# First gather of a deformable convolution: positions made in two halves, and the second image's table copy and normalized image stored later, from another queue

## The chip, the cores and the metric

The kernel runs on one core of a Trainium2 chip. The metric is device time in microseconds, from the launch of the program to its end. Engines are named as in the profile: PE is TensorE (PEld its weight loads), DVE is VectorE, ACT is ScalarE, POOL is GpSimd, SP is the sync engine, which here only issues transfers. SPq, ACTq and POOLq are the issuing sides of these engines.

## The reference

Four layers run one after another on an input of 4 images, 192 channels, 64x64 pixels, all in float32. The change touches the beginning of layer 0, a transformer block whose query is a 3x3 deformable convolution. Cut to that part:

```python
xs = x.reshape(B, C, H * W).transpose(0, 2, 1)
xn = layer_norm(xs, gamma1, beta1).transpose(0, 2, 1).reshape(B, C, H, W)
q = deform_conv(xn, w_p, b_p, w_d)
...
def deform_conv(x, w_p, b_p, w_d):
    off = conv2d(x, w_p, stride=1, pad=1) + b_p[None, :, None, None]
    xp = jnp.pad(x, ((0, 0), (0, 0), (1, 1), (1, 1)))
    ...
    px = off[:, :N].transpose(0, 2, 3, 1) + p0x + pn[0]
    py = off[:, N:].transpose(0, 2, 3, 1) + p0y + pn[1]
    fx, fy = jnp.floor(px), jnp.floor(py)
    ...
    xo = g_lt * gat(qlx, qly) + g_rb * gat(qrx, qry) + g_lb * gat(qlx, qry) + g_rt * gat(qrx, qly)
    return conv2d(xo, w_d, stride=KS, pad=0)
```

A small convolution gives every pixel two offsets for each of nine taps. At each of these nine places the normalized, padded image is read with bilinear weights from four neighbours, all 192 channels at once, and the result goes into a second convolution. The rest of layer 0 is channel attention and an MLP. Layer 1 is a non-local block, layer 2 a window attention block, layer 3 a small masked depthwise convolution.

## The kernel before, in words

**Order of the work.** One Python function describes all work as tiles and instructions. A scheduler then orders the instructions of each engine by their place in the program and by its own estimate of when operands are ready, and it sets the semaphores. Each engine runs its own list strictly in order. `in_turn(...)` (L174) pins a transfer behind the instruction that was described last for the same engine, so that the scheduler can't issue it earlier. Transfers that SP issues go out in SP's order, those that ACT issues in ACT's.

**Images.** Image 0 is prepared and gathered at the very beginning (L1948 to L1965). Its gather runs beside the making of constants (`constants`, L183) and beside the preparation of image 1 (`offsets(1, second, woven=True)`). Then follows the MLP of image 0 (`mlp0(0, ...)`, L1970). After it a loop over the four images runs layers 1, 2 and 3 of image b. Inside layer 1 of image b the gather of image b+1 is woven in, and inside layer 3's stage the MLP of image b+1. Images 2 and 3 are prepared at the start of layer 1 of the image before them (L1986).

**`offsets` (L436)** prepares one image in four steps:

- It normalizes the image in eight chunks into `xn` (96 partitions, two channel halves, a padded image of 66x66).
- `write_table` (L489) transposes pixels to rows and stores them into `table`, an array in DRAM with one entry of 2x192 floats for every padded pixel. The row of a pixel is stored twice: into columns C to 2C of its own entry (q = 1), and into columns 0 to C of the entry one image row (66 entries) later (q = 0). One entry then holds two pixels that stand above each other, and two entries in a row hold the four neighbours that the bilinear read needs. Image 0 and images 2 and 3 do this in 4 groups, image 1 in 8. Each group issues four stores on SP (two q by two image rows, L509). For image 0 the transposed rows also stay in SBUF in `kept`.
- After the groups, `xn` is stored as a whole to `xn_drams` (L512, 3270 KB). The MLP of that image reads it from there (`load_normalized`, L757).
- `convolve` (L514) computes the offsets in two halves of 16 tiles each (72 matmuls of 512 columns a half), and adds the grid into `pos` (L535). After both halves nine VectorE instructions (L544 to L556) clamp the positions, take floors, make the weights `pos` and `fr`, and make the index `idx`, each over all 32 tiles of 18 values.

Image 1 runs `convolve` before `write_table`, the others the other way round.

**`gather` (L559)** goes over five groups of taps (two, two, two, two, one), and in each over the 32 tiles. For each tile and tap POOL issues one indirect transfer (L616) that fetches 128 times four neighbours, 393 KB, into one of 11 slots of `ring`. Then ACT (L622), DVE (L623), ACT (L626), DVE (L627) interpolate, and PE multiplies `xo` with the unshifted row of the pixels (`kept`, or `ti` loaded from columns C to 2C of the table, L610). At the end come the second convolution, the attention matrix, and its product with the projection, `m2`; the last ACT instructions of it are the copies at L728 and L729.

**`mlp0` (L739)** then takes one pixel chunk after another: `attend`, the sum with the image, a layer norm whose squares ACT makes at L812, two matmul layers with a GELU between them.

**Buffers.** `xn`, `ring` and other large tiles share two buffers of the pool `big`; a new one waits until all readers of the one before are done, a store to DRAM too. There are two tables and two copies of `xn_drams`, used by even and odd images.

Of the kernel before, what the change touches and what calls it, by code (L numbers as in the profile page):

```python
# [13 lines left out]
ALU = mybir.AluOpType  # L14
# [67 lines left out]
def conv_seq_kernel(ctx: ExitStack, tc: tile.TileContext, a, out: bass.AP):  # L82
# [350 lines left out]
    def given(b):  # L433
        return a["x"][b].rearrange("(k p) h w -> p k (h w)", p=P)

    def offsets(b, pool, kept=None, woven=False):  # L436

# [16 lines left out]
        with ExitStack() as s:  # L456
            sb = s.enter_context(pool_of(name="l0a", bufs=1 if woven else 2))
            s1 = s.enter_context(pool_of(name="l0a1", bufs=1))
            ps = s.enter_context(pool_of(name="l0aps", bufs=2, space=PSUM))
            for i in range(NCH):  # L460
                xi = sb.tile([P, 2, CN], F32, tag="xi", name=f"xi_{b}_{i}", bufs=2)
                nc.sync.dma_start(out=xi, in_=given(b)[:, :, bass.ts(i, CN)])
                layer_norm(
                    xi, CN, xnv[:, :, 1 + 8 * i : 9 + 8 * i, 1:65], sb, ps, f"l0_{b}_{i}",
                    affine=(V["l0_g1"], V["l0_b1"]), rows=8,
                )
                yield

            wp = s1.tile([P, 2, 9, 32], F32, tag="wp", name=f"wp_{b}")
            given_wp = s1.tile([P, 2, 9, 18], F32, tag="given_wp", name=f"given_wp_{b}")  # L470
            nc.sync.dma_start(out=given_wp, in_=a["wp"].rearrange("(k p) t o -> p k t o", p=P))
            nc.gpsimd.memset(wp, 0.0)
            nc.gpsimd.tensor_copy(wp[:, :, :, 0:18], given_wp)
            bp = s1.tile([128, 1], F32, tag="bp", name=f"bp_{b}")
            nc.gpsimd.memset(bp, 0.0)
            for q in range(4):
                nc.sync.dma_start(out=bp[32 * q : 32 * q + 18, :], in_=a["bp"])
            p0 = s1.tile([128, NU, 18], F32, tag="p0", name=f"p0_{b}")
            for to, of, t in (((0, W), (0, W), 0), ((W, 2 * W - 2), (WP, 2 * W), 0), ((2 * W - 2, 2 * W), (0, 2), 1)):
                nc.sync.dma_start(out=p0[slice(*to), 0, :], in_=a["p0"][slice(*of), t, :])  # L480
            n = 1
            while n < NU:
                nc.gpsimd.tensor_scalar_add(p0[:, n : 2 * n, 0:9], p0[:, 0:n, 0:9], 2.0 * n)
                nc.gpsimd.tensor_copy(p0[:, n : 2 * n, 9:18], p0[:, 0:n, 9:18])
                n *= 2

            G, T = 4 if woven else 8, 4

            def write_table():  # L489
                for g in range(NU // G):  # L490
                    if kept is None:
                        tt = sb.tile([128, G, C], F32, tag="tt", name=f"tt_{b}_{g}", bufs=2)
                    else:
                        tt = kept[:, bass.ts(g, G)]
                    for j in range(G):
                        r0 = 2 * (g * G + j) + 1
                        pt = ps.tile([128, C], F32, tag="tr", name=f"pt_{b}_{g}_{j}")
                        for k in range(2):
                            for h in range(2):
                                nc.tensor.matmul(  # L500
                                    pt[bass.ts(h, W), bass.ts(k, P)], lhsT=xnv[:, k, r0 + h, 1 : W + 1], rhs=ident[:P, :P],
                                    start=True, stop=True,
                                )
                        nc.scalar.copy(tt[:, j, :], pt)
                    for q in range(2):
                        e = g * G * UT + (2 - q) * WP + 2
                        to = table[e : e + G * UT, bass.ts(q, C)].rearrange("(j r w) c -> r w j c", r=2, w=WP)
                        for h in range(2):
                            nc.sync.dma_start(out=to[h, 0:W], in_=tt[bass.ts(h, W)])  # L509
                    if not woven or g % 2 == 1:  # L510
                        yield
                nc.sync.dma_start(out=xn_drams[b % 2], in_=xn)  # L512

            def convolve():  # L514
                for g0 in range(0, NU // T, 4):
                    ng, m = 4, 128
                    po = ps.tile([128, T * 128], F32, tag="off", name=f"po_{b}_{g0}", bufs=1)
                    for tap in range(9):
                        for k in range(2):
                            for q in range(ng):  # L520
                                r0, c0 = (g0 + q) * 2 * T + tap // 3, tap % 3
                                nc.tensor.matmul(
                                    po[32 * q : 32 * q + 32].rearrange("p (r c) -> p r c", c=W), lhsT=wp[:, k, tap, :],
                                    rhs=xnv[:, k, r0 : r0 + 2 * T, c0 : c0 + W],
                                    start=tap == 0 and k == 0, stop=tap == 8 and k == 1,
                                )
                    ot = sb.tile([128, T * 128], F32, tag="ot", name=f"ot_{b}_{g0}")
                    nc.scalar.activation(ot[:m], po[:m], AF.Identity, bias=bp[:m])
                    pp = ps.tile([128, T, 4, 32], F32, tag="tr", name=f"pp_{b}_{g0}")
                    for j in range(T):  # L530
                        nc.tensor.transpose(
                            pp[:, j, 0:ng, :].rearrange("p q o -> p (q o)"), ot[:m, bass.ts(j, 128)], ident[:m, :m]
                        )
                    tiles = slice(g0 * T, (g0 + ng) * T)
                    nc.vector.tensor_tensor(  # L535
                        pos[:, tiles, :].rearrange("p (q j) o -> p j q o", j=T), pp[:, :, 0:ng, 0:18],
                        p0[:, tiles, :].rearrange("p (q j) o -> p j q o", j=T), ALU.add,
                    )
                    yield

            for part in (convolve(), write_table()) if woven else (write_table(), convolve()):
                yield from part

            nc.vector.tensor_scalar(pos, pos, -1.0, 65.0, ALU.max, ALU.min)  # L544
            fi = s1.tile([128, NU, 18], I32, name=f"fi_{b}", tag="fi")
            fl = s1.tile([128, NU, 18], F32, name=f"fl_{b}", tag="fl")
            nc.vector.tensor_copy(fi, pos)
            nc.vector.tensor_copy(fl, fi)
            nc.vector.tensor_tensor(fr, fl, pos, ALU.is_gt)
            nc.vector.tensor_tensor(fl, fl, fr, ALU.subtract)  # L550
            nc.vector.tensor_tensor(fr, pos, fl, ALU.subtract)
            nc.vector.tensor_scalar(pos, fr, -1.0, 1.0, ALU.mult, ALU.add)
            nc.vector.scalar_tensor_tensor(
                fl[:, :, 0:9], fl[:, :, 0:9], float(WP), fl[:, :, 9:18], ALU.mult, ALU.add
            )
            nc.vector.tensor_scalar(idx, fl[:, :, 0:9], 2.0, 2.0 * MID, ALU.mult, ALU.add)  # L556
        return pos, fr, idx

    def gather(b, s, at, m2, kept=None):  # L559
# [1387 lines left out]

    begun, at_second = ExitStack(), None  # L1948
    second = begun.enter_context(pool_of(name="l0second", bufs=1))
    with ExitStack() as s:  # L1950
        sb = s.enter_context(pool_of(name="l0first", bufs=1))
        m2 = stats.tile([M, C + 3 * M], F32, tag="m2", name="m2_0")
        kept = sb.tile([128, NU, C], F32, tag="kept", name="kept")
        at = links(offsets(0, sb, kept))
        beside = [constants(), offsets(1, second, woven=True)]
        for k, _ in enumerate(gather(0, s, at, m2, kept)):
            if k < 20 or not beside:
                continue
            if len(beside) == 2 and k % 4 == 0 or len(beside) == 1 and k % 13 == 0:
                try:  # L1960
                    next(beside[0])
                except StopIteration as end:
                    at_second = end.value
                    beside.pop(0)
        assert not beside  # L1965
    with ExitStack() as s:
        sb, pool = (s.enter_context(pool_of(name=n, bufs=1)) for n in ("norms0", "l0d0"))
        ps = s.enter_context(pool_of(name="l0dps", bufs=2, space=PSUM))
        wide = s.enter_context(pool_of(name="l0dps2", bufs=5, space=PSUM))
        for _ in mlp0(0, m2, pool, sb, Psums({"n": ps, "v": ps, "h": wide})):  # L1970
            pass
# [117 lines left out]
```

## Time and profile before

| | us |
|---|---|
| median of 4 runs | 6745.02 (6739.23 to 6752.7) |
| the profiled execution | 6748.98 |
| its span, first to last instruction | 6747.2 |
| preparation of image 0, up to the first gather | 0 to 123.9 |
| gather of image 0, first to last issue | 123.9 to 609.0 |
| its end, up to the last copy into `m2` | 609.0 to 643.4 |
| MLP of image 0 | 642.5 to 837 |
| first gather of image 1, inside layer 1 of image 0 | 841.5 |
| first gathers of images 2 and 3 | 2483.1 and 4057.4 |

The table is read off the timeline of the profiled execution. Some groups of its page that belong to the gather (line, engine, operation, output and input, how many over the whole run; then busy us and mean ns, and idle us before them with what ended most of it):

```profile
L616 POOL DMA_INDIRECT ring<-table,idx x1152 | 1634.4, 1419 | 1149.3 <-issue 221.1
L622 ACT ACTIVATE row<-ring,pos 128x384 f32<-128x384 f32 x1152 | 671.9, 608 | 202.9 <-DVE xo L627 106.3
L623 DVE SCALAR_TENSOR_TENSOR row<-ring,fr,row 128x384 f32<-128x384 f32 x1152 | 675.1, 613 | 93.9 <-ACT row L622 64.8
L634 PE MATMUL h<-kept,xo 128*128 128x192 f32 x960 | 249.2, 396 | 125.5 <-DVE xo L627 79.9
```

A quarter of each of the first three counts belongs to image 0. In the tables of stretches that follow below, the DMA share is the mean busy share of the core's 16 DMA engines and the clock the mean share of full speed that TensorE was granted.

### The profile page before, as it was taken

The numbers are of one execution on the slowest core, as the hardware profiler recorded it, in microseconds if no ns is written. First come the engines' busy times: TensorE is split into PE (matmuls) and PEld (weight loads), VectorE is DVE, ScalarE is ACT, GpSimd is POOL, SyncE is SP. The second block draws the span as 40 slices with busy tenths as digits, with TensorE's granted clock in tenths as the row PEclk, the third lists the DMA queues.
The fourth block names the chain that finished last, engine by engine and source line by source line (L and its number), as shares of the span: only waits on it lengthen the run. The fifth ranks groups of instructions, "written<-read, shape, count | busy, mean of one in ns | idle before, by whom it ended". The sixth has DMA issues, their size and how long they took to land. (4 is left out here: it accounts for less than half of the span.)

```text
span 6747.2 us, 115790 instructions
## 1 busy us (share of the span) xinstructions
PE 6161.1 (91%) x45392; PEld 4185.5 (62%) x45392; DVE 4694.2 (70%) x6908; ACT 3599.4 (53%) x6136; POOL 2064.2 (31%) x2276
## 2 busy tenths in 40 slices
PE   8687999999989899999998899999998989999897
PEld 4445577787644457887654447878664457776533
DVE  3664269886586849996576858988467777765667
ACT  3664358774445347885445337877344435544332
POOL 2654047661200027773210006765220000002200
PEclk8788989999999999999999999999998999999998
DMA  6785156662010156663110046666101010001000
GB/s 181 254 283 187 51 159 214 207 207 61 10 43 15 32 177 208 219 205 116 35 29 23 20 124 210 218 200 186 38 9 43 15 57 11 15 14 36 5 7 21
DMA packets 330496, 699.37 MB, mean 104 GB/s; under 512 B 60077, under 2 KB 217181, under 8 KB 329182
## 3 DMA queue, kind: packets, MB, share of 16 engines
q0 software_dynamic: 92736, 455.22, 20.7%
q1 hardware_dynamic: 236382, 235.95, 12.1%
q8 instruction: 358, 5.87, 0.4%
q14 instruction: 188, 1.54, 0.1%
q10 hardware_dynamic: 832, 0.79, 0.0%
HBM read 611.25 MB, written 78.87 MB: 102 GB/s over the span
## 5 line engine op out<-in xcount | busy, mean ns | idle before, releaser
L616 POOL DMA_INDIRECT ring<-table,idx x1152 | 1634.4, 1419 | 1149.3 <-issue 221.1
L963 PE MATMUL s<-ths,ph 96*128 96x256 f32 x4096 | 990.8, 383 | 4.7 <-ACT ths L957 2.4
L963 PEld LDWEIGHTS s<-ths,ph 96*128 96x128 f32 x4096 | 784.3, 193 | 132.0 <-ACT ths L957 5.1
L622 ACT ACTIVATE row<-ring,pos 128x384 f32<-128x384 f32 x1152 | 671.9, 608 | 202.9 <-DVE xo L627 106.3
L1031 PE MATMUL y<-sc,gx 128*97 128x256 f32 x3008 | 724.4, 382 | 24.3 <-ACT yn L1037 19.0
L623 DVE SCALAR_TENSOR_TENSOR row<-ring,fr,row 128x384 f32<-128x384 f32 x1152 | 675.1, 613 | 93.9 <-ACT row L622 64.8
L1031 PEld LDWEIGHTS y<-sc,gx 128*97 128x97 f32 x3008 | 492.2, 165 | 157.4 <-ACT yn L1037 20.8
L626 ACT ACTIVATE xo<-row,pos 128x192 f32<-128x192 f32 x1152 | 486.2, 448 | 155.7 <-remote 73.3
L627 DVE SCALAR_TENSOR_TENSOR xo<-row,fr,xo 128x192 f32<-128x192 f32 x1152 | 446.8, 412 | 120.2 <-ACT xo L626 81.9
L1028 DVE TENSOR_TENSOR sc<-sc,mbs 128x1024 f32<-128x1024 f32 x376 | 453.4, 1218 | 58.1 <-issue 31.0
L965 ACT COPY sc<-s 128x1024 f32<-128x1024 f32 x376 | 377.2, 1003 | 178.3 <-PE s L963 141.0
L634 PE MATMUL h<-ti,xo 128*128 128x192 f32 x2304 | 439.1, 330 | 0.0
L970 DVE TENSOR_TENSOR top<-top,sc 128x1024 f32<-128x1024 f32 x282 | 344.4, 1221 | 135.0 <-ACT sc L965 114.3
L1029 ACT ACTIVATE sc<-sc 128x1024 f32<-128x1024 f32 x376 | 393.6, 1053 | 77.4 <-DVE sc L1028 69.6
L634 PEld LDWEIGHTS h<-ti,xo 128*128 128x128 f32 x2304 | 392.6, 191 | 29.1 <-issue 8.2
L1180 DVE TENSOR_REDUCE es<-ex 128x6 f32<-128x384 f32 x264 | 133.3, 546 | 367.0 <-ACT ex L1176 367.0
L634 PE MATMUL h<-kept,xo 128*128 128x192 f32 x960 | 249.2, 396 | 125.5 <-DVE xo L627 79.9
L634 PEld LDWEIGHTS h<-kept,xo 128*128 128x128 f32 x960 | 180.7, 221 | 216.1 <-DVE xo L627 111.5
L1377 DVE SCALAR_TENSOR_TENSOR ga<-gate,v,ga 128x1024 f32<-128x1024 f32 x234 | 300.4, 1284 | 6.7
L1624 POOL COPY gate<-gate 128x192 f32<-128x192 f32 x12 | 4.2, 348 | 975.5 <-ACT gate L1617 846.4
L1031 PE MATMUL y<-se,gx 128*97 128x256 f32 x1088 | 272.1, 392 | 10.7 <-ACT se L1029 10.2
L858 ACT ACTIVATE gl<-h,bias_fc 128x256 f32<-128x256 f32 x384 | 150.8, 473 | 236.0 <-PE h L851 235.6
(391 smaller groups left out, 11223.6 us busy)
## 6 DMA issues: line engine op xcount, KB each, us to landing
ti<-table SPq DMA_DIRECT2D x768, 48.0 KB
ring<-table,idx POOLq DMA_INDIRECT x1152
xnd<-xn SPq DMA_DIRECT2D x4, 3270.0 KB
xi<-in_x_dram SPq DMA_DIRECT2D x32, 384.0 KB
xk<-xd SPq DMA_DIRECT2D x32, 384.0 KB
xd<-xc SPq DMA_DIRECT2D x64, 192.0 KB
table<-tt SPq DMA_DIRECT2D x32, 384.0 KB
xc<-xd SPq DMA_DIRECT2D x60, 192.0 KB
```

The source lines that it names most:

```text
L616: nc.gpsimd.indirect_dma_start(out=gt.rearrange("p q r c -> p (q r c)"), out_offset=None, in_=corners, in_offset=bass.IndirectOffsetOnAxis ...
L622: nc.scalar.activation(row, gt[:, 0], AF.Copy, scale=pos[:, t, 9 + tap : 10 + tap])
L623: nc.vector.scalar_tensor_tensor(row, gt[:, 1], fr[:, t, 9 + tap : 10 + tap], row, ALU.mult, ALU.add)
L626: nc.scalar.activation(xo[:, j, :], row[:, 0, :], AF.Copy, scale=pos[:, t, tap : tap + 1])
L627: nc.vector.scalar_tensor_tensor(xo[:, j, :], row[:, 1, :], fr[:, t, tap : tap + 1], xo[:, j, :], ALU.mult, ALU.add)
L634: nc.tensor.matmul(acc[m // 2][:, bass.ts(m % 2, C)], lhsT=xo.rearrange("p j c -> p (j c)")[:, bass.ts(m, 128)], rhs=tt, start=t == 0 and ...
L963: nc.tensor.matmul(p[:, t, :], lhsT=ph[:, bass.ts(G * g + t, 128)], rhs=ths[i], start=True, stop=True)
L965: nc.scalar.copy(to, p)
L970: nc.vector.tensor_tensor(tops[i], tops[i], to, ALU.max)
L1028: nc.vector.tensor_tensor(ex, ex, mbs[i].unsqueeze(1).to_broadcast([128, G, QN]), ALU.add)
L1029: nc.scalar.activation(ex, ex, AF.Exp)
L1031: nc.tensor.matmul(py, lhsT=gx[:, G * g + t, :], rhs=ex[:, t, :], start=g == 0 and t == 0, stop=g == NG - 1 and t == G - 1,)
```

## The change

It has three parts, all in `offsets` and where it is called.

- **Positions in halves.** The nine instructions become a function of a range of tiles. Images 0, 2 and 3 call it after each half of the convolution with the 16 tiles of that half, image 1 once for all, as before.
- **The store of `xn`.** For image 0 it is cut into four, one behind each group's table stores. For image 1 it isn't made in `offsets` any more but appended to a list, `later`. For images 2 and 3 it stays.
- **The table of image 1.** Only the columns C to 2C are stored from SBUF (16 stores in place of 32). The columns 0 to C are filled by four copies from DRAM to DRAM, 1056 rows of 192 floats each, also in `later`.

When the gather of image 0 has been described, the five transfers of `later` are issued from ACT, each pinned with `in_turn`.

```diff
-    def offsets(b, pool, kept=None, woven=False):
+    def offsets(b, pool, kept=None, woven=False, later=None):
...
-                    for q in range(2):
+                    for q in range(1 if later is not None else 0, 2):
                         e = g * G * UT + (2 - q) * WP + 2
                         to = table[e : e + G * UT, bass.ts(q, C)].rearrange("(j r w) c -> r w j c", r=2, w=WP)
                         for h in range(2):
                             nc.sync.dma_start(out=to[h, 0:W], in_=tt[bass.ts(h, W)])
+                    if kept is not None:
+                        of = slice(g * G * UT, (g + 1) * G * UT if (g + 1) * G < NU else XNW)
+                        nc.sync.dma_start(out=xn_drams[b % 2][:, :, of], in_=xn[:, :, of])
                     if not woven or g % 2 == 1:
                         yield
-                nc.sync.dma_start(out=xn_drams[b % 2], in_=xn)
+                if kept is not None:
+                    return
+                if later is None:
+                    nc.sync.dma_start(out=xn_drams[b % 2], in_=xn)
+                    return
+                later.append((xn_drams[b % 2], xn))
+                for g in range(0, NU * UT, NU * UT // 4):
+                    e = g + WP + 2
+                    to, of = (slice(at, at + NU * UT // 4) for at in (e + WP, e))
+                    later.append((table[to, 0:C], table[of, C : 2 * C]))
...
-            for part in (convolve(), write_table()) if woven else (write_table(), convolve()):
-                yield from part
-
-            nc.vector.tensor_scalar(pos, pos, -1.0, 65.0, ALU.max, ALU.min)
             fi = s1.tile([128, NU, 18], I32, name=f"fi_{b}", tag="fi")
             fl = s1.tile([128, NU, 18], F32, name=f"fl_{b}", tag="fl")
-            nc.vector.tensor_copy(fi, pos)
...
+
+            def positions(tiles):
+
+                p, q, i, l, n = (t[:, tiles, :] for t in (pos, fr, fi, fl, idx))
+                nc.vector.tensor_scalar(p, p, -1.0, 65.0, ALU.max, ALU.min)
+                nc.vector.tensor_copy(i, p)
+                nc.vector.tensor_copy(l, i)
+                nc.vector.tensor_tensor(q, l, p, ALU.is_gt)
+                nc.vector.tensor_tensor(l, l, q, ALU.subtract)
+                nc.vector.tensor_tensor(q, p, l, ALU.subtract)
+                nc.vector.tensor_scalar(p, q, -1.0, 1.0, ALU.mult, ALU.add)
+                nc.vector.scalar_tensor_tensor(l[:, :, 0:9], l[:, :, 0:9], float(WP), l[:, :, 9:18], ALU.mult, ALU.add)
+                nc.vector.tensor_scalar(n, l[:, :, 0:9], 2.0, 2.0 * MID, ALU.mult, ALU.add)
+
+            if woven:
+                yield from convolve()
+                yield from write_table()
+                positions(slice(0, NU))
+            else:
+                yield from write_table()
+                for k, _ in enumerate(convolve()):
+                    positions(bass.ts(k, NU // 2))
+                    yield
...
+    later = []
...
-        beside = [constants(), offsets(1, second, woven=True)]
+        beside = [constants(), offsets(1, second, woven=True, later=later)]
...
         assert not beside
+        for to, of in later:
+            in_turn(nc.scalar.dma_start(out=to, in_=of))
```

More of the change, by code (lines that the diff above doesn't have):

```diff
@@ L539, in convolve @@
                     yield
-            for part in (convolve(), write_table()) if woven else (write_table(), convolve()):
-                yield from part
-            nc.vector.tensor_scalar(pos, pos, -1.0, 65.0, ALU.max, ALU.min)
             fi = s1.tile([128, NU, 18], I32, name=f"fi_{b}", tag="fi")
             fl = s1.tile([128, NU, 18], F32, name=f"fl_{b}", tag="fl")
-            nc.vector.tensor_copy(fi, pos)
[L548 to L556, printed above, removed]
+            def positions(tiles):
[18 more added lines that the diff above has]
+                    yield
         return pos, fr, idx
```

## The prediction

> **What bounds the kernel now.** I read the page first, then the timeline of the first 700 us by engine, then tables of short stretches.
>
> ```profile
> span 6747.2 us, 115790 instructions
> PE 6161.1 (91%) x45392; PEld 4185.5 (62%) x45392; DVE 4694.2 (70%) x6908; ACT 3599.4 (53%) x6136; POOL 2064.2 (31%) x2276
> ```
>
> TensorE bounds the whole, but the change touches the first 650 us, which have limits of their own. In this table of stretches the first row is the first gather as a whole, the second the stretch behind the second image's normalized store, the last four part of that image's table stores (columns: stretch, length, busy PE, PEld, DVE, ACT, POOL, clock, DMA share, GB/s).
>
> ```profile
> 124.00:616.00 492.00, 355.27 (x1776) 229.76 (x1777) 299.75 (x629) 295.45 (x651) 307.31 (x329) 0.82 0.81 265
> ```
>
> ```profile
> 400.00:410.00 10.00, 9.22 (x45) 2.98 (x40) 2.93 (x7) 3.23 (x7) 2.42 (x3) 1.00 0.98 357
> ...
> 444.00:454.00 10.00, 6.71 (x64) 5.14 (x62) 8.40 (x18) 6.38 (x17) 7.38 (x8) 1.00 0.95 311
> 454.00:464.00 10.00, 8.37 (x51) 6.02 (x52) 5.20 (x12) 5.97 (x16) 4.90 (x6) 0.53 1.01 344
> 464.00:474.00 10.00, 9.94 (x63) 7.43 (x61) 4.84 (x10) 6.53 (x17) 4.90 (x5) 0.62 0.81 254
> 474.00:484.00 10.00, 5.72 (x53) 4.01 (x52) 4.85 (x11) 5.70 (x16) 5.74 (x6) 1.00 1.02 361
> ```
>
> No compute engine is full in this gather, and where stores run beside it the DMA share is near 1 while VectorE, ScalarE and POOL fall off: those stretches are DMA-bound. Between them 288 gathers take 492 us, 1.7 us each, though POOL can issue one each 1.25 us (0.95 and a gap of 0.30).
>
> The start of that stage, in the timeline (start, length, instruction, idle before and its releaser):
>
> ```profile
> 94.32 11.43 SPq L509 DMA_DIRECT2D table<-kept  x4
> 97.38 0.46 DVE L535 TENSOR_TENSOR pos<-pp,p 128x288 f32<-128x288 f32 x1 [7.75 <-issue]
> 114.45 0.46 DVE L535 TENSOR_TENSOR pos<-pp,p 128x288 f32<-128x288 f32 x1 [16.61 <-PE pp L531]
> 119.46 0.21 DVE L240 COPY wide<-p_wide 128x46 f32<-128x46 f32 x1 [3.57 <-PE p_wide L238]
> 123.31 0.31 DVE L556 TENSOR_SCALAR idx<-fl 128x288 int32<-128x288 f32 x1
> 123.92 1.22 POOL L616 DMA_INDIRECT ring<-table,idx  x1 [108.24 <-DVE idx L556]
> ```
>
> The first gather waits for the last index; half of the positions were there 26 us earlier, and VectorE then idled 16.61 us.
>
> **Part A, positions in halves (gain, taken as 15).** The first half's nine operations can start at 97.84. At full size they cost 0.46+0.46+0.45+3x0.76+0.46+0.45+0.31 = 4.87 us; half of them costs between 2.4 and 4.9, and by the 128x288 rows (0.31 and 0.45-0.46) some 3.2, so the indices stand at 101. The table is the next thing late. The third group's four stores were issued at 78.70 and the DMA share fell to 0.19 in 86-88, so a group takes some 7.7 us. The fourth group's are issued at 94.32 and are held 11.43 us behind the 3270 KB store of the normalized image that SP issued at 90.62. In the change that store is cut into four of 818 KB, three of them out in idle DMA time behind the earlier groups (shares 0.08 in 72-80 and 0.09 in 86-90), so the fourth group lands near 102-103. First gather at 103 instead of 123.92: 21 us. Three more stores on SP at 0.32 each, in its idle time, cost nothing; without that cover 1 us. The later nine operations stand on VectorE behind the second convolution half (114.45), with row work of the gather behind them, while POOL runs up to 11 slots ahead. Part of the lead is given back: in 106-124 the DMA carried weights and constants (shares 0.56 to 1.04, 13 us of full work), and TensorE the 5.25 us of L238 and 5.28 of L215 besides the convolution; these now lie beside gathers. Between all of it hidden (21) and nothing left (0) I take 15, as gathers at 126-136 still went out 9 in 10 us at a DMA share of 0.88.
>
> **Part B, second image's normalized store out of the gather (gain, taken as 6).** Issued at 392.10, it is followed by this:
>
> ```profile
> 401.18 0.94 POOL L616 DMA_INDIRECT ring<-table,idx  x1 [0.30 <-issue]
> 409.40 0.94 POOL L616 DMA_INDIRECT ring<-table,idx  x1 [7.27 <-DMA ring<-table,idx]
> ```
>
> 3270 KB at the 357 GB/s of that stretch are 9.4 us, POOL's wait is 7.3; some of the wait may return elsewhere. Bounds 0 and 9.
>
> **Part C, half of its table stores gone (gain, taken as 7).** 16 of 32 stores of 192 KB, 3.1 MB at the mean 314 GB/s of 444-504, are 10 us of a saturated stretch. VectorE waited there for ScalarE rows, and ScalarE once 2.8 us for a store that held a buffer. Bounds 0 and 10.
>
> **Part D, images three and four (gain, taken as 3).** They also get halves. Their first gathers (2483.13, 4057.41) follow the index (2481.94, 4056.23) within 1.2 us; ScalarE then idles 2.48 us for gathered rows. The tables are still landing around 2470, so a few us at most are to be had, beside layer 1 work that keeps PE at 0.97. Bounds -1 (nine more short VectorE instructions) and 8.
>
> **Part E, five transfers on ScalarE's queue behind the gather (loss, taken as 20).** They are pinned behind ScalarE's last traced instruction, the copies into m2:
>
> ```profile
> 643.21 0.21 ACT L729 COPY m<-pm 64x64 f32<-64x64 f32 x1
> 650.63 0.84 ACT L812 ACTIVATE sq_l0m<-d_l0m 128x768 f32<-128x768 f32 x1 [7.21 <-DVE d_l0m L796]
> 651.49 1.28 ACT L362 ACT_TABLE_LOAD   x1
> ```
>
> Their sources are complete by then, so they don't wait for data. But an issue holds its engine when the queue is full:
>
> ```profile
> 78.70 4.66 SPq L509 DMA_DIRECT2D table<-kept  x4
> 90.62 0.32 SPq L512 DMA_DIRECT2D xnd<-xn  x1
> ```
>
> Alone an issue takes 0.3 to 0.6 us. Four of 512 rows each were accepted 4.66 us after the first, with about half of their 2048 rows moved: so some 1000 rows of 768 bytes fit ahead. Behind the long store four took the 11.43 shown above. The new set is that store and 4x1056 rows from DRAM to DRAM, for which this trace has no row. The store is 11 us (the shares of 90-110 sum to 17.2 us, less 6.2 for 2048 table rows). A copied row costs at least the 3.0 ns of a table row (6.2 us/2048) and at most a write and a read at that price, 6.0; I take 4.0, nearer the store, which is the nearest row. ScalarE is free when 1000 rows are left: 643.4+1+11+3224x0.0040 = 668.3; with 3.0 it is 665, with 6.0 it is 675. The squares, wanted at 650.63, come 18 us late (14 to 24; 0 if nothing holds). Behind them wait the table load, the root, VectorE's reciprocal and all matmuls of the first MLP tile, on a stage where PE is busy 98% in 660-840: nothing takes it back. SP's loads for the next tile (647.35, with a wait of 1.14 us on them) share the DMA engines with the copies, but the held squares are later still. The readers of what moves are far off: the second gather starts at 841.48, the second image's normalized loads at 1894.6. PE idles meanwhile; after its idle 4.43 us before 638.02 the granted clock was 0.50 in 636-644 and 0.78 in 644-648. Half speed for some 4 us adds 2: 20 in all.
>
> The Trainium skill ("DMA: Bandwidth & Descriptors", section "Issuing engines are not separate DMA queues") says that transfers started by different engines share the same 16 DMA engines, and that spreading the issues saves only sequencer time, usually little: it would make E near 0, where the 11.43 us row says sequencer time is not little. The same page's Specifications give 358 GB/s of HBM to a core; copies that read and write 3.24 MB there would take an estimated 18 us instead of 16.9, one us more in E. Stretches of this trace reach 361 and 369 GB/s, so the limit isn't sharp here.
>
> **Sum.** -15-6-7-3+20 = -11. The profiled execution took 6748.98 us (span 6747.2 and 1.8 around it), 4.0 above the median 6745.02 of the four runs. So 6738 by the profiled one, and 6734 against the median: the forecast.
>
> **Rivals.** *One: the copies hold nobody.* If ScalarE's queue takes all five at 0.6 us, the 3 us vanish in its 7.21 us of idle time: -31, 6714. For it: the DMA share in 636-648 is 0.00. Against it: SP's held issues, and 4224 rows are four times what SP had accepted ahead. *Two: no lead at the front.* Either the first gather still waits for all indices (against it: stores of `kept` slices went out at 35.6 while later slices were written until 94.3, so waits follow slices), or the constants' loads and L238/L215 in front of the gather's matmuls eat it. A is then 3: -19+20 = +1, 6746. *Three, slower: DRAM-to-DRAM rows are slow.* Place: ScalarE between 643 and its first squares. To lose more than parts A to D gain by 13.5 the hold must cost 44.5, release at 693, that is from 11.7 ns a row, 3.9 times the table row; at 16 ns: release 707, loss 58, sum +27, 6772. For it: no such copy in the trace; a read that must finish before each write. Against it: 768-byte loads and stores run at like rates here.
>
> **How the numbers follow.** What a measurement can tell here is about 0.2%, 13.5 us. Forecast 0.48, rival one 0.20, two 0.12, three 0.20. The forecast's own range by its bounds is 6719 to 6749; 40% of it lies below 6731.5. Faster: 0.19+0.20+a little of two = 0.41; slower: 0.20 and 0.02 of the others; same 0.37. The range from 6711 to 6761 leaves out most of rival three and the ends.
>
> **What would show it.** First gather at 102-105 and its first index from the half-size L556; POOL without a 7 us wait near 400; DMA share below 0.9 in the table stretch; the last gather of image one 25-30 us earlier; ScalarE's five issues taking some 25 us together, first squares 25 us after the m2 copies instead of 7. A hold under 8 us or over 45 would make the prediction wrong, as would a gather that starts early and ends no earlier.

## The result, and the profile after

The changed kernel takes 6754.17 us (median of 40 runs, 6721.56 to 6779.04); the kernel before, in 66 runs that were taken beside it, 6732.09 us. The ratio is 1.0036, 95% interval 1.0025 to 1.0047: 24 us slower, where 11 us faster was forecast. (6754 lies inside the range that was given, since the four runs shown with the kernel before were 13 us above its later median; the direction is wrong all the same.)

The page of the profiled execution, first line and engines:

```profile
span 6751.5 us, 115799 instructions
PE 6144.6 (91%) x45392; PEld 4185.3 (62%) x45392; DVE 4696.4 (70%) x6935; ACT 3598.8 (53%) x6136; POOL 2074.9 (31%) x2276
```

Totals show nothing; the change is in the first 700 us. The front in the timeline (start, length, instruction, idle before and its releaser):

```profile
86.25 0.46 DVE L547 TENSOR_TENSOR pos<-pp,p 128x288 f32<-128x288 f32 x1 [7.75 <-issue]
89.82 0.23 DVE L567 TENSOR_SCALAR idx<-fl 128x144 int32<-128x144 f32 x1
97.18 1.22 POOL L637 DMA_INDIRECT ring<-table,idx  x1 [81.43 <-DMA v<-in_v_dram]
114.32 0.20 DVE L240 COPY wide<-p_wide 128x46 f32<-128x46 f32 x1 [7.84 <-PE p_wide L238]
116.47 0.23 DVE L567 TENSOR_SCALAR idx<-fl 128x144 int32<-128x144 f32 x1
116.74 1.63 ACT L643 ACTIVATE row<-ring,pos 128x384 f32<-128x384 f32 x3 [13.07 <-DVE idx L567]
118.28 1.08 POOL L637 DMA_INDIRECT ring<-table,idx  x1 [7.22 <-DVE row L644]
```

The first gather is out at 97.18, earlier than forecast. But ScalarE, which makes the first row of a gathered tile, does nothing until the second half's index is done (116.47 and 0.23 long), and when the 11 slots of the ring are full POOL waits too. In the kernel before the first row stood at 127.99.

The end of the gather and the start of the MLP:

```profile
606.10 38.89 SPq L776 DMA_DIRECT2D xa<-in_x_dram  x3
629.70 0.36 ACTq L1989 DMA_DIRECT2D xnd<-xn  x1
630.24 0.21 ACT L750 COPY m<-pm 64x64 f32<-64x64 f32 x1
645.35 1.49 SPq L781 DMA_DIRECT2D xb<-xnd  x3
648.09 2.04 PE L787 MATMUL o<-xb,m 128*128 128x512 f32 x2 [18.46 <-DMA xb<-xnd]
649.43 6.14 ACTq L1989 DMA_DIRECT2D table<-table  x4
657.26 0.84 ACT L833 ACTIVATE sq_l0m<-d_l0m 128x768 f32<-128x768 f32 x1 [26.82 <-DMA table<-table]
662.85 2.07 PE L787 MATMUL o<-xb,m 128*128 128x512 f32 x2 [7.18 <-DMA xb<-xnd]
```

Three loads of the MLP's first tile are spread over 38.89 us. In the kernel before they took 1.74:

```profile
619.13 1.74 SPq L755 DMA_DIRECT2D xa<-in_x_dram  x3
```

The table of waits of SP says for what the changed kernel's loads waited (waiter, releaser, us in total, times, longest):

```profile
SPq L776 <- DMA xnd<-xn: 37.2, 1, 37.2
```

SP's third load waited for the *store* that ScalarE had still to issue. The two share no data: the load fills `xa` from the input, the store empties `xn`. What they share is a completion counter. In the program each transfer of SP and ScalarE is given one of eight such counters (0 to 7 here), and waits until the transfer that had it before has landed. In the list of the changed program's instructions with what each waits for, the two (ScalarE's, then SP's) read as follows; DMAHW0 is counter 0:

```
L1989 DMACopy xnd_122<-xn_1800 96x2x4360 [waits DMAHW0_49]
L776 DMACopy xa_0_4286<-in_x_dram 64x256 [waits DMAHW0_49]
```

The store, pinned behind the copies into `m2`, had counter 0 first, so the load could not go out before the store had landed. It landed near 644.1 by its last packet; the load was issued at 644.5.

### The profile page after: what moved, and what is told of

It reads as the page before. It is cut to its first block, busy times and chain, and to the rows that moved or that the text cites. A ratio compares the mean times of both kernels' runs of the same rounds, so it can differ in the third digit from the quotient of the medians.

```text
span 6751.5 us, 115799 instructions
## 1 busy us (share of the span) xinstructions
PE 6144.6 (91%) x45392; PEld 4185.3 (62%) x45392; DVE 4696.4 (70%) x6935; ACT 3598.8 (53%) x6136; POOL 2074.9 (31%) x2276
## 4 chain that ended last, share of the span: by engine, by line
PE 38%; DVE 12%; issue 3%; ACT 3%; DMA 1%; POOL 0%; SPq 0%; DVEq 0%; ACTq 0%; POOLq 0%; another core or an unknown queue 0%
PE y L1052 7%; PE s L984 6%; PE h L655 2%; PE v L1217 2%; PE h L1595 1%; DVE ha L1398 1%; PE qk L1142 1%; PE qk L1143 1%; PE t L1225 1%; DVE ga L1398 1%; DVE gate L1398 1%; PE rb L1291 1%; PE s L1178 1%; PE h L1597 1%; PE zm L1607 1%
```

## The experiments

Time is given as a ratio to the kernel before on the same chip. The chips differ: on two of them the kernel before took 6595 us, on two others 6768 to 6773 (the faster and the slower kind below). The squares are ScalarE's first work on an MLP tile; the last copy into `m2` is ScalarE's last step ahead of the MLP.

| run | ratio | interval | last m2 copy to first squares, us | first to second squares, us |
|---|---|---|---|---|
| before, 3 profiles (the first one, b0 at 6773, b1 at 6768) | | | 7.4, 7.9, 7.6 | 12.1 |
| changed kernel, first measurement | 1.0036 | 1.0025 to 1.0047 | 27.0 | 20.0 |
| a0, changed, chip with 6773 | 1.0025 | 1.0003 to 1.0047 | 27.0 | 19.8 |
| a1, changed, chip with 6768 | 1.0037 | 1.0014 to 1.0061 | 27.3 | 19.6 |
| x1, halves only, 6595 | 0.9982 | 0.996 to 1.0003 | 7.1 | 12.1 |
| x2, late transfers only, 6595 | 1.0006 | 0.9986 to 1.0027 | 26.6 | 19.0 |
| x3, late from SP, 6595 | 0.9973 | 0.9954 to 0.9993 | 7.3 | 12.1 |
| x4, late from POOL, 6595 | 0.9968 | 0.9947 to 0.9988 | 7.8 | 12.1 |
| x4b, the same, 6596 | 0.9965 | 0.9944 to 0.9986 | 8.2 | 12.1 |
| x6, only the store late, 6596 | 0.9998 | 0.9976 to 1.002 | 27.3 | 12.5 |
| x7, only the copies late, 6596 | 1.0009 | 0.9987 to 1.0031 | 25.7 | 15.5 |
| x10, late, ahead of the chain, 6596 | 0.9996 | 0.9977 to 1.0014 | 6.7 | 12.1 |
| x8, x4 with floors apart, 6773 | 0.9998 | 0.9977 to 1.002 | 7.0 | 13.6 |
| x8b, the same, 6768 | 1.0005 | 0.9977 to 1.0033 | 7.1 | 13.5 |
| x9, late from POOL, no halves, 6773 | 1.0009 | 0.9988 to 1.0031 | 6.9 | 12.1 |
| x13, x8 with constants behind, 6768 | 1.0003 | 0.9982 to 1.0025 | 7.1 | 13.5 |

**The parts apart.** x1 leaves out the late transfers:

```diff
-        beside = [constants(), offsets(1, second, woven=True, later=later)]
+        beside = [constants(), offsets(1, second, woven=True)]
```

> The halves and the split store of image 0 stay; image 1's table and normalized image are stored as before, nothing comes later. Theory (the late transfers cost, by a completion counter that SP's loads of the first MLP tile share with the store): the 27 us between the last copy into m2 and the second MLP tile go, first squares 7 us after the last copy into m2, and the time is 12 us under before plus what images 3 and 4 lose or gain: ratio 0.997 to 0.999. Rival (the halves themselves cost, in the front or in images 3 and 4): ratio 1.001 or more although the squares come 7 us after the copies.

x2 keeps them and makes all positions at once; image 0's normalized image is stored whole again:

```diff
-                    if kept is not None:
-                        of = slice(g * G * UT, (g + 1) * G * UT if (g + 1) * G < NU else XNW)
-                        nc.sync.dma_start(out=xn_drams[b % 2][:, :, of], in_=xn[:, :, of])
...
-                for k, _ in enumerate(convolve()):
-                    positions(bass.ts(k, NU // 2))
-                    yield
+                yield from convolve()
+                positions(slice(0, NU))
```

> The late transfers alone; positions of all images made whole and image 0's normalized image stored whole, as before. Theory (counter): SP's third load of the first MLP tile is issued when the store on ScalarE's queue lands, some 15 us after that is issued; first squares 25 to 27 us after the last copy into m2; against that the gather of image 0 gets what the stores took from it, 0 to 13 us: ratio 1.002 to 1.004. Rival (late transfers harmless, the halves cost): ratio 0.998 or less.

Without the late transfers the squares follow at 7.1 us, with them alone at 26.6: the hold belongs to them. x2's whole time, though, came out at 1.0006, below what was expected; on this chip the gather won more than I had allowed for (numbers under B and C in the next section).

**Whose queue.** The same transfers, issued by SP in x3; in x4 and x4b, which are one kernel on two chips, `nc.gpsimd` stands there for POOL:

```diff
-            in_turn(nc.scalar.dma_start(out=to, in_=of))
+            in_turn(nc.sync.dma_start(out=to, in_=of))
```

> The changed kernel with the five late transfers issued from SP, where they come directly behind image 1's last table store (some 500 us in). Theory (counter): no load of the MLP waits for a transfer that another engine has yet to issue; first squares 7 us after the last copy into m2, the gather of image 0 pays up to 20 us of transfer time for it at 500 to 550; ratio to before 0.996 to 1.000. Rival (the copies' own traffic costs the 27 us wherever it lies): the gather's last issue moves back by 20 us or more and the ratio stays at 1.003.

> The changed kernel with the five late transfers issued from POOL, whose transfers have completion counters of their own; the store goes out before the last gather steps, the copies behind them, near 595. Theory (counter): SP's loads are not held, the transfers run under the 27 us chain behind the gather, first squares 7 to 10 us after the last copy into m2: ratio 0.996 to 0.999. Rival (ScalarE's queue is not the point, the copies' traffic is): MLP inputs late by 15 us or more, ratio 1.002 or more.

> The late transfers from POOL once more, on whatever chip this is: where the gather's stage is DMA-bound at 390 GB/s it was 0.9968. Theory: squares 7 to 8 us after m2 on any chip, and the ratio 0.996 to 1.000; 24 us under the changed kernel, which measured 1.0025 and 1.0036.

Same bytes, same rows, and the hold is gone in all three. From SP they are issued from 435.8 on, still in the gather, and the last is accepted at 476.4; from POOL behind it, under the chain that makes `m2`:

```profile
543.40 0.71 POOL L1989 DMA_DIRECT2D xnd<-xn  x1
...
545.26 3.09 POOL L1989 DMA_DIRECT2D table<-table  x4 [0.29 <-issue]
```

(timeline of x4). POOL's transfers have counters of their own, so no load of SP waits for them. The copies' own traffic costs nothing that can be seen at the first tile there. Its ratio of 0.9968 and 0.9965 is the best of the study, on chips with 6595 us; as it stands it was not run on the slower ones.

**Which transfer holds.** x6 leaves only the store late, and both columns of image 1's table are stored from SBUF:

```diff
-                    for q in range(1 if later is not None else 0, 2):
+                    for q in range(2):
...
-                for g in range(0, NU * UT, NU * UT // 4):
-                    e = g + WP + 2
-                    to, of = (slice(at, at + NU * UT // 4) for at in (e + WP, e))
-                    later.append((table[to, 0:C], table[of, C : 2 * C]))
```

x7 leaves only the copies late:

```diff
-                later.append((xn_drams[b % 2], xn))
+                nc.sync.dma_start(out=xn_drams[b % 2], in_=xn)
```

> Of the late transfers only the store of the normalized image is left on ScalarE's queue; image 1's table is stored from SBUF in both halves as before. Theory (counter): SP's third load of the first MLP tile waits on the counter of the store and goes out when it lands, 12 to 15 us after the last copy into m2; first squares 19 to 22 us behind that copy in place of 26.6, the second tile 12 us after the first in place of 19. Rival (the copies' traffic makes the 26.6): squares 7 to 10 us after the copy. Time to before: 1.000 to 1.002.

> Only the four copies within DRAM are left late, on ScalarE's queue; the normalized image of image 1 is stored as before. Now SP's second and third load of the first MLP tile share counters with the second and third copy. Theory (counter): these loads wait until those copies land, some 8 to 12 us after the last copy into m2; first squares 15 to 22 us behind it. Rival (ScalarE held by its queue, as the prediction had it): the copies' issues take 10 us or more together and the squares follow their end at once. Time to before: 1.000 to 1.002.

Timeline of x6, then of x7:

```profile
545.41 38.89 SPq L772 DMA_DIRECT2D xa<-in_x_dram  x3
569.02 0.35 ACTq L1985 DMA_DIRECT2D xnd<-xn  x1
596.90 0.84 ACT L829 ACTIVATE sq_l0m<-d_l0m 128x768 f32<-128x768 f32 x1 [27.14 <-DVE d_l0m L813]
```

```profile
556.16 30.59 SPq L128 DMA_DIRECT2D fc<-scaled_fc  x2
580.91 0.56 ACTq L1989 DMA_DIRECT2D table<-table  x1
586.79 5.19 SPq L776 DMA_DIRECT2D xa<-in_x_dram  x3
607.15 0.84 ACT L833 ACTIVATE sq_l0m<-d_l0m 128x768 f32<-128x768 f32 x1 [25.50 <-DVE d_l0m L817]
```

The store alone, one issue of 0.35 us, makes the whole 27 us at the first tile, where the kernel before has 7.4 to 7.9. So neither the copies' traffic nor a held ScalarE is needed for it. I had expected 19 to 22: the release came 15 us after the issue, as expected, but from there to the squares it takes 13 us, not the 4 to 7 that were left for it, at a mean clock of 0.64. What the copies add in the changed kernel is the second tile, 20 us behind the first in place of 12: its loads stand in the DMA engines among the rows of the copies (DMA share in 650 to 660 0.99, before 0.37), and SP waits 3.8 us in all on the counters of two weight loads ahead of them. In x7 one more counter is shared than I had read: already a load of weights ahead of `xa` (L128) has the first copy's counter, and its two transfers are spread over 30.59 us.

**Is ScalarE held by its queue, as I had predicted?** x10 keeps ScalarE and issues the five behind the last gathered row:

```diff
+            if k == 288:
+                assert not beside
+                for to, of in later:
+                    in_turn(nc.scalar.dma_start(out=to, in_=of))
...
-        for to, of in later:
-            in_turn(nc.scalar.dma_start(out=to, in_=of))
```

> All five late transfers on ScalarE's queue as in the changed kernel, but issued behind the last row of the gather, before the 27 us chain that makes m2, and so ahead of one copy into hs. Theory (counter): the store lands 12 to 15 us after the gather, SP's loads go out then and are there when m2 is; first squares 7 to 10 us after the last copy into m2. If ScalarE's queue holds it, the copy into hs behind the transfers is late by what the hold takes (0 by the 6 us that four issues took, up to 20 by the prediction's reckoning). Time to before 0.997 to 1.002.

```profile
534.68 0.36 ACTq L1982 DMA_DIRECT2D xnd<-xn  x1
536.04 17.71 ACTq L1982 DMA_DIRECT2D table<-table  x4
553.79 0.48 ACT L661 COPY hs<-h 128x384 f32<-128x384 f32 x1 [17.32 <-DMA table<-table]
```

(timeline of x10). Yes, when nothing else parts them: ScalarE is held 19.1 us from the store's issue on, where my working would give 24.9 (643.4 to 668.3). The counters of these copies were last used by transfers that SP had issued some 90 us earlier, so this is no wait on a counter. It is not free either: from the last gathered row to the last copy into `m2` x10 takes 51.5 us, all other runs 30.1 to 33.8. In the changed kernel this never came about. There the copies first waited 19 us for a counter that a load of SP had, the store was gone by then, and four issues took 6.14 us. They were over at 655.57, before the squares had their input near 657.2.

**Why the first rows wait.** In x8, and in x8b, the same kernel on another chip, the late transfers come from POOL, and the second half's floors lie in a buffer that outlives the gather (fi, fl are two tiles each, one a half; image 1 calls `positions` twice):

```diff
+            fls = [(p if kept is not None and k else s1).tile([128, NU // 2, 18], F32, name=f"fl{k}_{b}", tag=f"fl{k}") for k, p in enumerate((s1, pool))]
```

> The late transfers from POOL, and the second half's floors (fi, fl) put into a buffer that lives as long as the gather; the first half's stay. Image 1 makes its positions in two calls. Theory (the first rows of the gather wait for the second half's index since they are written where fl lay): ScalarE's first row at 100 to 104 in place of 117, POOL's 11 slots come free without the 7 to 9 us wait near 112, up to 12 us won: ratio 0.995 to 0.997. Rival (the rows wait for something else, or PE's wait for the constants at 152 takes all): the first row stays behind the last index, or the lead is gone by the 48th gather; ratio as with the late transfers from POOL alone, 0.997.

> Late transfers from POOL and the second half's floors in a buffer of their own, once more: first row at 100 to 104, 15 us ahead of the changed kernel's, and by the 36th row 5 us or less of it left, as PE waits near 150 for the second folded matrix. Ratio to before 0.999 to 1.000 on a chip of the slow kind, 0.995 to 0.997 on a fast one.

```profile
102.78 0.62 ACT L645 ACTIVATE row<-ring,pos 128x384 f32<-128x384 f32 x1
...
146.04 5.25 PE L215 MATMUL p_fc1T<-v,w_fc1T 96*128 96x1 f32 x24 [7.22 <-DMA w_fc1T<-in_fc1T_dram]
```

(timeline of x8, ScalarE and TensorE). The first row moves from 118.0 (a0, same chip) to 102.8; with POOL as the issuer alone (x4) it stands at 117.9. So that was the cause: the gather's tiles are written where the floors lay, and the floors are read until the last index. The whole time did not follow: 0.9998 and 1.0005, where 0.995 to 0.997 was expected of x8. The second line shows what is late next: TensorE reaches the folding of the second matrix (one of the constants) and waits for its load. The changed kernel has the same wait, the kernel before has none (timeline of b0, then of the changed kernel; the clock in 50 to 70 was 1.00 in both):

```profile
129.47 0.34 SPq L211 DMA_DIRECT2D w_fc1T<-in_fc1T_dram  x1
142.70 5.25 PE L215 MATMUL p_fc1T<-v,w_fc1T 96*128 96x1 f32 x24 [0.83 <-issue]
148.12 0.17 DVE L218 TENSOR_TENSOR bias_fc1T<-p_fc1T,v 128x6 f32<-128x6 f32 x1 [5.27 <-PE p_fc1T L215]
```

```profile
140.05 0.34 SPq L211 DMA_DIRECT2D w_fc1T<-in_fc1T_dram  x1
151.83 5.25 PE L215 MATMUL p_fc1T<-v,w_fc1T 96*128 96x1 f32 x24 [9.34 <-DMA w_fc1T<-in_fc1T_dram]
157.12 0.16 DVE L218 TENSOR_TENSOR bias_fc1T<-p_fc1T,v 128x6 f32<-128x6 f32 x1 [14.41 <-PE p_fc1T L215]
```

So it is VectorE that stops: in its order L218 stands ahead of the row work, and it idles 14.41 us there in place of 5.27. And the load itself goes out 10.6 us later, behind 25 gathers in place of 12. In x2 and x9, which have no halves, it goes out at 129.6 and 129.3, in the runs with halves between 134.8 and 152.0. The gathers that the halves let out early lie in front of the constants' loads: the DMA share in 112 to 120 is 1.03 in the changed kernel and 0.45 in b0. That this traffic is what delays the load is read from these rows; no run tested it alone.

x13 begins the constants at gather step 36 and pins these matmuls behind the gather's:

```diff
+                        if name == "fc1T" and m == k == 0:
+                            in_turn(mm)
...
-            if k < 20 or not beside:
+            if k < 36 or not beside:
...
-            if len(beside) == 2 and k % 4 == 0 or len(beside) == 1 and k % 13 == 0:
+            if len(beside) == 2 and k % 2 == 0 or len(beside) == 1 and k % 13 == 0:
```

> As the one before, and the constants begin at gather step 36 in place of 20 (and step twice as often), with the matmuls of the second folded matrix (fc1T) pinned in TensorE's order behind the gather's matmuls described before them. Theory (these matmuls, waiting in TensorE's order for a load that lands near 150, take the lead of an earlier first row): the 24th row at 145 to 152 in place of 157 to 163, 10 us or more of the lead left at the 48th row, 5 to 12 us under the kernel without the pin. Rival (DMA is the limit there, whatever TensorE waits for): the 48th row comes when it came before.

Start of ScalarE's work on gathered row 0, 48, 144 and the last, on the chip with 6768 us: before 128.2, 212.9, 372.9, 619.7; changed 117.9, 208.6, 366.7, 602.8; x8b 105.2, 200.2, 359.9, 605.0; x13 106.8, 188.6, 362.9, 602.4. The pin does save 12 us by the 48th row. None of them is left at the 144th, and the whole time is the same within the intervals (1.0003 and 1.0005), where 5 to 12 us less was expected. What takes them there was not settled. (b1, the kernel before on this chip, was expected to begin its rows near 117.8 as b0 did. It began at 128.2, with a clock of 0.61 in 50 to 70.)

**Halves or not, with the hold gone.** x9 is x2 with POOL as the issuer.

> The late transfers from POOL and positions made whole for all images, image 0's normalized image stored whole: the change without its first part and without its hold. Theory (halves worth some 10 us): 0.998 to 1.000, 5 to 12 us above the same with halves (0.9968). Rival (halves worth nothing, the gather runs into the same fixed points): 0.996 to 0.997.

x9, without halves, takes 1.0009, above both ranges that were expected; x8 with halves and floors apart takes 0.9998 on the same chip: no difference that these intervals show. The changed kernel itself was run again, unchanged, on each of the two chips:

> The changed kernel once more, beside its variants. Theory (counter): 25 to 27 us lie between the last copy into m2 and the second MLP tile that before doesn't have; late transfers alone gave 1.0006 and halves alone 0.998, so here the sum of the parts would be 0.999, the first measurement 1.0036. If it is 1.002 or more again, the parts do not add and the halves and the late transfers cost each other something; if it is near 1.000, what differs is the chip.

> The changed kernel on this chip. Theory: 26 to 27 us between the last copy into m2 and the first squares on any chip; against that the gather of image 0 wins 0 to 5 us where the DMA moves 360 GB/s in its stretches and 20 to 25 where it moves 390. So 1.0025 to 1.0036 on a chip of the first kind, 0.999 to 1.002 on one of the second.

It is 1.0025 and 1.0037 on two chips, so the first measurement stands. By what was put down for a0, this would mean that the parts do not add. But x1 and x2 ran on a chip with 6595 us and the changed kernel never did, so a difference between the chips would explain it as well. What speaks for the chips is x9: without halves and without the hold it gains nothing that can be told from 0 on the slower kind, while x2 gained enough on the faster kind to pay for its hold. The two were not separated.

## Why the prediction was wrong

**Its sum was -15-6-7-3+20.** Three profiles of each kernel, before then changed, give in its place: the last gather of image 0 at 609.0, 600.1 and 615.8, then 595.4, 603.7 and 598.4, that is 9 us earlier for parts A, B and C together (28 forecast); from the last copy into `m2` to the first GELU 18.1, 18.5 and 18.3, then 45.6, 45.4 and 45.5, that is 27 us lost in part E (20 forecast). -9+27 = +18, and the gather of image 1 begins 17 us later (842 and 859 in the mean). The ratios give +17 to +25. What came is the prediction's own sign of being wrong, a gather that starts early and ends hardly earlier.

**A, the step that failed most: "Between all of it hidden (21) and nothing left (0) I take 15".** That is, of the first gather's lead. The first gather came at 97.2 to 98.6, so the steps up to it held: nine operations in 3.3 us (3.2 forecast), the last table group earlier since the store was cut. But I followed the lead only as far as POOL. The first row could not be written before the floors were dead, and I had not asked where the gather's tiles lie: ScalarE's first row came at 116.7 to 118.0. Then the constants: I had priced L215 at its 5.28 us, not the load ahead of it, which the early gathers put off, nor VectorE's order behind it (14.41 us idle in place of 5.27). Rival two named these loads, and on A it was right. The base was also one draw of several: of three profiles of the kernel before, two had a clock of 0.61 in 50 to 70 and a first gather at 124, the third full clock there and 113.8. Against that one A is worth nothing: first row at 117.8 before, 116.7 to 118.0 after, and A, B and C together 1 us at the last gather (600.1 before, 599.2 in the mean after) in place of 9.

**B and C were right in place and near in size, but shortened the gather by little on these chips.** The table of stretches after:

```profile
400.00:410.00 10.00, 9.99 (x58) 4.54 (x58) 6.29 (x15) 5.55 (x13) 7.56 (x9) 0.94 0.88 291
444.00:454.00 10.00, 8.74 (x59) 6.92 (x60) 7.32 (x15) 7.50 (x20) 5.64 (x5) 0.66 0.77 231
454.00:464.00 10.00, 7.82 (x63) 4.96 (x62) 5.74 (x15) 6.17 (x17) 5.13 (x5) 0.93 0.95 310
```

The DMA share falls (0.98 to 0.88, 0.95 to 0.77, 1.01 to 0.95). ScalarE's waits for gathered rows, behind the first one's, fall from 27.8, 28.3 and 31.6 us in the three profiles before to 16.7, 13.9 and 18.8 after: 13 us, the sum of B and C. In the same profiles its waits for rows that VectorE works on rise from 13.1, 15.4 and 13.6 to 29.6, 28.7 and 28.0. Tables of waits of ScalarE, before and after:

```profile
ACT row L622 <- DMA ring<-table,idx: 27.8, 31, 4.4
ACT xo L626 <- DVE row L623: 13.1, 20, 4.9
```

```profile
ACT row L643 <- DMA ring<-table,idx: 16.7, 18, 1.8
ACT xo L647 <- DVE row L644: 29.6, 24, 14.0
```

One wait of 13 to 14 us makes nearly all of the rise, the one during which VectorE stands before the second folded matrix. It belongs to the halves: in x9, without them, these waits sum to 17.2. So A took back inside the stage what B and C gave. From first row to last the stage takes 485, 487 and 492 before, 483, 490 and 485 after, and 481 in x9, which has B and C without A (487 in b0, same chip). On the chips with 6595 us it is another matter: there 450 with neither part (x1), 428 with B alone (x6), 440 with C alone (x7), 419 to 430 with both (x2, x4, x4b, x10), single executions each, so 20 to 31 us where 13 were forecast.

**D, forecast 3, is not seen.** From the last gather of image 1 to the first of image 2 the three profiles before take 952.8, 954.2 and 949.7 us, those after 957.5, 951.2 and 963.7. From image 2 to image 3 it is 949.6, 951.2 and 956.9, then 946.0, 949.9 and 955.7.

**E was near in size and wrong in its mechanism: "their sources are complete by then, so they don't wait for data. But an issue holds its engine when the queue is full".** The hold by a full queue exists (x10), yet the loss was made by SP, not by ScalarE: a load was tied to a store by a shared counter and so to ScalarE's pin. The squares came 19 to 20 us late, where 18 were forecast, and the forecast's sign for E ("first squares 25 us after the m2 copies") came true at 27: luck, as another wait made them. I had written that SP's loads share the DMA engines with the copies "but the held squares are later still", and so put that at nothing; SP was the one held, and the copies cost the other 7 us (the first GELU 38.4 us behind `m2` in x6, 45.4 to 45.6 with the copies). Rival three, the slower one, had its place right and not its cause. Its price per row is refuted: the four copies, issued from 649.43 on, had landed by 666.3 by their last packets, 16.9 us for 4224 rows, 4.0 ns a row beside other loads, which is the value the prediction took.

The Trainium skill ("DMA: Bandwidth & Descriptors", section "Issuing engines are not separate DMA queues") makes the choice of the issuing engine a matter of sequencer time, usually small. Here the same five transfers took 27 us from ScalarE and nothing visible from POOL, and 17.3 us of ScalarE's own time in x10. Its other half, that transfers of all issuing engines run on the same 16 DMA engines and interleave, agrees: beside the copies the second tile comes 20.0 us behind the first, without them (x6) 12.5.

## What to carry to other kernels

Before a transfer is moved to another queue and pinned there, look in the program which completion counter it gets and which transfers come next on that counter: a late pin on one engine stops another engine's loads that have nothing to do with it. A queue with counters of its own and an idle engine (POOL here) took this late work at no cost that could be seen. A lead at the head of a chain counts only as far as it is followed: ask for each consumer in turn where its buffers lay before, what its engine has in order ahead of it, and what the early work now delays.

## What was not expected of the hardware

The same kernel took 6595 us on two chips and 6770 on two others (6732 in the first measurement). The rate of the DMA engines does not tell the kinds apart, as the expectation of a1 has it: stretches of ten us reach 387 and 393 GB/s in x3, on one of the first, but 388 in the profile before and in b0 too. On the slower kind ScalarE waits 30 to 73 us in this stage for something with no record in the trace (named "remote"), on the other kind not at all:

```profile
ACT xo L626 <- remote: 68.9, 11, 16.2
```

(table of waits of the kernel before, 130 to 613.) On the faster kind ScalarE's waits for DMA, for gathered rows and for the table's stores, fall from 75 us (x1) to 58 (x4b), 17 of the 30 us by which the stage shortens. Whether the waits without a record are what keeps the slower kind from gaining as much is not shown, and what they are stays open. So does which kind of chip a kernel will meet: the changed kernel lost 0.25 to 0.37% on the slower kind and was not run on the other, where x2, which has the same hold, lost nothing that can be told from 0.
